# 64-column products between 32-column attention sums: two column groups in place of four

## The chip, the cores and the metric

The kernel runs on one core of a Trainium2 chip. The time is the device time of one execution in microseconds, the median of several runs; less is better. The engines are named as the profile names them: PE is TensorE's matmul and PEld its weight load, DVE is VectorE, ACT ScalarE, POOL GpSimd, SP SyncE.

## The reference

An input x of shape (2, 256, 128, 128), f32: two batches, 256 times T, 128 bands FB, 128 channels C. Three steps, each added to x:

```python
xt = _ln(x, ln_t_w, ln_t_b).transpose(0, 2, 1, 3)
x = x + _mha(xt, t_wi, t_bi, t_wo, t_bo, H_T, cm).transpose(0, 2, 1, 3)   # over time, causal
xf = _ln(x, ln_f_w, ln_f_b)
x = x + _mha(xf, f_wi, f_bi, f_wo, f_bo, H_F, bm)                         # over bands, |i - j| <= 16
xn = _ln(x, ln_n_w, ln_n_b)
h = jax.nn.gelu(xn @ w1.T + b1, approximate=False)                        # 128 -> 512
x = x + (h @ w2.T + b2)                                                   # 512 -> 128
```

`_mha` has 4 heads of 32 channels: `qkv = x @ wi.T + bi`, softmax of scaled and masked scores, times v, and an output product with `wo`.

## The kernel before

All of the work is done in groups of 512 tokens (four tiles of 128): 128 groups over time (class `OverTime`), 128 over bands (`OverBands`) and 128 of the feed-forward part (`FeedForward`). First come all groups over time; then sixteen runs, each of eight groups over bands followed by eight of the feed-forward part.

A group has normalized and transposed tokens `xnT` (128 channels on the partitions, 512 tokens). Its matmuls, all in f32:

- `queries_keys` makes queries and keys, weights `wf` in the array, 512 tokens moving (in the profile `bank<-xnT,wf`).
- `values` makes values, the tokens in the array and `wf` moving, 128 columns for each tile (`bank<-wf,xnT`). Over time, tiles 1 and 3 (`swapped`) have the two halves of their tokens exchanged, by the argument `turn`.
- the scores of a head use 32 rows and 64 columns of the array (`bank<-qT,kT`); over time in an order written out by hand, over bands with 80 moving columns for each 64 keys.
- `weigh` makes the sums of the softmax with a block of ones (`bank<-p,ones` over time, `bank<-pf,ones` over bands) and the weighted values (`bank<-p,v`, `bank<-pf,v`), 128 rows and 32 columns, each head in its own 32 columns.
- `output` makes the output product with `wn` (`bank<-wn,oT`), 128 moving columns a tile.
- in the feed-forward part `hidden` multiplies by `w1f` (512 moving, `bank<-xnT,w1f`) and `weigh` by `w2T_sb` (128 moving, `bank<-w2T_sb,hT`), summed over four parts of the hidden layer.

Queries, keys, values, outputs and both feed-forward products go through one helper, `product`. It writes 128 output partitions in several matmuls side by side, each into a part of the array's columns, with all 128 rows.

Each engine has one queue, worked off in the order in which the program issues (`InOrder` pins it); the loop in `BoundedPath.run` writes that order out. Stages of neighbouring groups are interleaved. In a step over time PE does: the scores of two groups, the output product of an earlier one, sums and weighted values of another, projections of a later one, and the scores again. In a step over bands: scores, sums, weighted values, output product, projections, scores. A feed-forward step has hidden products, second products and hidden products again; its first steps still finish the last band groups, its last ones start the next run's.

PSUM has eight banks, handed on by number (`bank_108` to `bank_115` in the order below). A second path, `shifted_path`, is for inputs whose scores could be too large for a softmax without a maximum; it isn't executed on this input.

All the instructions are issued by one wrapper, so the profile puts nearly all of them on its line, L907: tile names, not lines, tell them apart.

Of the kernel before, what the change touches and what calls it, by code (L numbers as in the profile page):

```python
# [19 lines left out]
P = 128  # L20
H = 4
D = 32
# [3 lines left out]
NT = 4  # L26
# [7 lines left out]
HALF = P // 2  # L34
# [335 lines left out]
class Group:  # L370
# [150 lines left out]
    def values(self):  # L521
        pass
# [38 lines left out]
class Attention(Group):  # L561
# [9 lines left out]
    def queries_keys(self):  # L571
        path = self.path
        wf = path.k.wf[self.which]
        self.qp = path.bank([P, NT * P], "qp", self.place.get("qp", path.held.pop("qp", None)))
        product(path, self.qp, wf[:, 0:P], self.xnT)

        self.kp = path.bank([P, NT * P], "kp", self.place.get("kp"))
        product(path, self.kp, wf[:, P : 2 * P], self.xnT)
# [11 lines left out]
    def values(self):  # L590
        path = self.path
        wv = path.k.wf[self.which][:, 2 * P : 3 * P]
        self.vp = path.bank([P, NT, P], "vp", self.place.get("vp"))
        for i in range(NT):
            product(path, self.vp[:, i], self.xnT[:, i * P : (i + 1) * P], wv, turn=2 if i in self.swapped else 0)

    def take_values(self):
        path = self.path
# [43 lines left out]
def rows_of(h):  # L642
    return slice(h * D, (h + 1) * D)


def product(path, out, weights, x, start=True, stop=True, turn=0):


    for c in range(P // D):
        path.tensor.matmul(out[rows_of(c)], weights[:, rows_of((c + turn) % NT)], x, start=start, stop=stop)  # L650


class OverTime(Attention):
# [7 lines left out]
    def values(self):  # L661
        path = self.path
        wv = path.k.wf[self.which][:, 2 * P : 3 * P]
        self.vp = [path.bank([P, 2, P], "vp", self.place.get(f"vp{s}")) for s in range(2)]
        for i in range(NT):
            product(
                path, self.vp[i // 2][:, i % 2], self.xnT[:, i * P : (i + 1) * P], wv, turn=2 if i in self.swapped else 0
            )

    def take_values(self):  # L670
# [842 lines left out]
```

## Time and profile before

| | |
|---|---|
| median of 3 runs | 2633.39 us (2633.3 to 2634.98) |
| span of the profiled execution, first to last instruction | 2631.9 us |
| what lies around the span, against the lowest run | 1.4 us |
| PE busy | 2617.8 us (99%), 68688 matmuls |
| PE weight loads busy | 1837.4 us (70%), 68688 loads |
| DVE / ACT / POOL busy | 2140.8 (81%) / 1838.8 (70%) / 1958.6 (74%) us |
| granted TensorE clock, mean | 1.000 |

No time of its own is listed for the profiled execution besides its span, so the span stands beside the runs. Busy time is the time in which at least one instruction of an engine or group is running; matmuls overlap, so the busy times of groups add up to more than the engine's. A mean duration is that of one instruction from its start to the end of its results, with the way through the array; how fast matmuls follow one another is read from the starts in the timeline, where instructions of one kind in a row are merged. A form such as 128\*32 is rows\*columns of the array that an instruction uses.

### The profile page before, as it was taken

To read this page: it belongs to the slowest core of one execution; us is meant where nothing else is said; L and a number is where in the kernel's file an instruction comes from. 1 tells how busy PE (TensorE), PEld (TensorE's weight loads), DVE (VectorE), ACT (ScalarE), POOL (GpSimd) and SP (SyncE) were. 2 spreads that over 40 slices of the span, in tenths; PEclk is the share of its full clock that TensorE was granted. 3 is DMA by queue.
4 is the path that set the end of the run, shared out by engine and by line. 5 is a ranking of instruction groups with operands and counts; after the bars stand their busy time and mean duration, and the time that the engine had idled before them with its cause. 6 is when DMAs were issued, how large, how long until landed. Compare 5 with 4: busy or idle time off the path is not lost.

```text
span 2631.9 us, 156460 instructions
## 1 busy us (share of the span) xinstructions
PE 2617.8 (99%) x68688; PEld 1837.4 (70%) x68688; DVE 2140.8 (81%) x6410; ACT 1838.8 (70%) x3543; POOL 1958.6 (74%) x2311
## 2 busy tenths in 40 slices
PE   9999999999999999999999999999999999999999
PEld 6666666666766767666777776667676677777776
DVE  8888888888888887977878779788797797887974
ACT  7989988999899875564655746647557466475573
POOL 7999999999999987666667666665776666757762
PEclk9999999999999999999999999999999999999999
DMA  6656555565565454445454544554454445554543
GB/s 155 167 149 158 149 149 149 155 155 149 149 158 149 122 127 119 115 123 127 118 124 124 123 122 117 126 128 120 122 126 120 120 119 131 123 120 123 123 104 88
DMA packets 469797, 344.97 MB, mean 131 GB/s; under 512 B 43120, under 2 KB 404464, under 8 KB 469104
## 3 DMA queue, kind: packets, MB, share of 16 engines
q1 hardware_dynamic: 468408, 334.41, 50.5%
q8 instruction: 540, 8.85, 1.5%
q14 instruction: 153, 1.25, 0.2%
q10 hardware_dynamic: 696, 0.46, 0.1%
HBM read 167.98 MB, written 166.72 MB: 127 GB/s over the span
## 4 chain that ended last, share of the span: by engine, by line
PE 99%; DVE 0%; issue 0%; DMA 0%; ACT 0%; ACTq 0%; DVEq 0%
PE bank L907 99%; DMA x<-in_x 0%; DVE xh L907 0%; DVE bank L907 0%; DVE res L907 0%; DVE stats L907 0%; DVE oT L907 0%; DVE u L907 0%; DVE xnT L907 0%; ACTq L907 0%; ACT p L907 0%; DVE vy L907 0%; ACT lnv L907 0%; DVE mv L907 0%; ACT root L907 0%
## 5 line engine op out<-in xcount | busy, mean ns | idle before, releaser
L907 ACT ACTIVATE hT<-bank,b 128x512 f32<-128x512 f32 x512 | 348.1, 688 | 524.2 <-PE bank L907 483.2
L907 POOL TENSOR_SCALAR_AFFINE_SELECT pf<-pf 128x512 f32<-128x512 f32 x768 | 477.7, 637 | 185.3 <-ACT pf L907 159.1
L907 PEld LDWEIGHTS bank<-w2T_sb,hT 128*32 128x32 f32 x16384 | 467.4, 110 | 54.8 <-issue 29.0
L907 PE MATMUL bank<-xnT,wf 128*32 128x512 f32 x4096 | 492.4, 592 | 0.5 <-DVE xnT L907 0.5
L907 PE MATMUL bank<-xnT,w1f 128*32 128x512 f32 x4096 | 486.3, 592 | 0.2 <-issue 0.2
L907 PE MATMUL bank<-w2T_sb,hT 128*32 128x128 f32 x16384 | 482.8, 273 | 1.0 <-issue 1.0
L907 ACT ACTIVATE p<-bank 128x512 f32<-128x512 f32 (+1 forms) x1024 | 430.6, 494 | 62.9 <-PE bank L907 62.9
L907 DVE TENSOR_SCALAR xh<-x,mv,rstd 128x160 f32<-128x160 f32 (+1 forms) x1012 | 394.3, 432 | 59.7 <-POOL rstd L907 49.4
L907 POOL TENSOR_SCALAR_AFFINE_SELECT p<-p 128x1024 f32<-128x1024 f32 (+2 forms) x384 | 364.5, 949 | 57.5 <-ACT p L907 49.1
L907 PEld LDWEIGHTS bank<-wf,xnT 128*32 128x32 f32 x8192 | 243.3, 110 | 144.1 <-issue 101.6
L907 POOL TENSOR_TENSOR p<-p,p 128x512 f32<-128x512 f32 x256 | 324.6, 1291 | 10.6
L907 DVE BATCH_NORM_STATS2 stats<-x 128x6 f32<-128x128 f32 x1536 | 329.0, 276 | 3.4 <-DMA x<-in_x 3.4
L907 POOL TENSOR_SCALAR rstd<-mv 128x4 f32<-128x4 f32 x251 | 57.8, 230 | 361.7 <-DVE mv L907 360.5
L907 PEld LDWEIGHTS bank<-xnT,w1f 128*32 128x32 f32 x4096 | 183.6, 110 | 171.6 <-issue 109.6
L907 PE MATMUL bank<-qT,kT 32*64 32x80 f32 (+4 forms) x16384 | 302.0, 271 | 0.1
L907 PEld LDWEIGHTS bank<-qT,kT 32*64 32x64 f32 x16384 | 260.0, 131 | 51.2 <-ACT kT L907 50.6
L907 DVE TENSOR_TENSOR res<-bank,res 128x512 f32<-128x512 f32 (+1 forms) x259 | 170.3, 658 | 153.3 <-PE bank L907 144.7
L907 ACT ACTIVATE pf<-bank 128x512 f32<-128x512 f32 x512 | 265.8, 602 | 35.5 <-PE bank L907 31.3
L907 PE MATMUL bank<-wn,oT 128*32 128x128 f32 x8192 | 283.8, 274 | 0.1
L907 DVE STREAM_TRANSPOSE z<-xh 128x512 f32<-128x512 f32 x380 | 270.3, 711 | 13.3
L907 PE MATMUL bank<-wf,xnT 128*32 128x128 f32 x8192 | 276.5, 273 | 0.0
L907 POOL TENSOR_TENSOR rstd<-rstd,mhalf 128x4 f32<-128x4 f32 x251 | 260.8, 1039 | 20.9
(100 smaller groups left out, 3820.3 us busy)
## 6 DMA issues: line engine op xcount, KB each, us to landing
turned<-z SPq DMA_DIRECT2D x1520, 64.0 KB, 2.7
xnT<-turned SPq DMA_DIRECT2D x380, 256.0 KB, 3.2
x<-res SPq DMA_DIRECT2D x256, 128.0 KB, 2.5
x<-x SPq DMA_DIRECT2D x128, 256.0 KB, 4.1
out<-res SPq DMA_DIRECT2D x252, 128.0 KB, 2.3
x<-in_x SPq DMA_DIRECT2D x124, 256.0 KB, 4.3
x<-in_x SPq DMA_DIRECT2D x4, 128.0 KB, 2.8
x<-in_x SPq DMA_DIRECT2D x6, 64.0 KB, 2.9
```

The lines of the kernel that those rows point to most:

```text
L907: return self.tc.keep_in_program_order(emit(*args, **kwargs))
```

## The change

`product` splits its 128 output columns into two halves of 64 in place of four quarters of 32, and so issues two matmuls where it issued four. With two halves the exchange of token halves is `turn=1` in place of `turn=2`; which tokens land where stays the same. Sums, weighted values and scores have matmuls of their own and keep their forms.

```diff
@@ Attention.values @@
-            product(path, self.vp[:, i], self.xnT[:, i * P : (i + 1) * P], wv, turn=2 if i in self.swapped else 0)
+            product(path, self.vp[:, i], self.xnT[:, i * P : (i + 1) * P], wv, turn=1 if i in self.swapped else 0)
@@ product @@
-    for c in range(P // D):
-        path.tensor.matmul(out[rows_of(c)], weights[:, rows_of((c + turn) % NT)], x, start=start, stop=stop)
+    for c in range(2):
+        w = (c + turn) % 2
+        path.tensor.matmul(
+            out[c * HALF : (c + 1) * HALF], weights[:, w * HALF : (w + 1) * HALF], x, start=start, stop=stop
+        )
@@ OverTime.values @@
-                path, self.vp[i // 2][:, i % 2], self.xnT[:, i * P : (i + 1) * P], wv, turn=2 if i in self.swapped else 0
+                path, self.vp[i // 2][:, i % 2], self.xnT[:, i * P : (i + 1) * P], wv, turn=1 if i in self.swapped else 0
```

The order of the stages stays as it was on every engine of the executed path; what changes is which matmuls PE finds in it. PE's order in a step over time, before, from the end of the scores to the start of the next ones (out<-in, output partitions x moving columns, how many in a row):

```order
L907 MATMUL bank_115<-qT,kT 64x64
L907 MATMUL bank_108<-wn_236,oT 32x128 x16
L907 MATMUL bank_114<-p_6843,ones 32x2x128 x4
L907 MATMUL bank_114<-p_7001,ones 32x2x128 x4
L907 MATMUL bank_113<-p_6843,v 32x256 x4
L907 MATMUL bank_113<-p_7001,v 32x128 x4
...
L907 MATMUL bank_109<-xnT,wf_151 32x512 x4
L907 MATMUL bank_112<-xnT,wf_151 32x512 x4
L907 MATMUL bank_108<-wf_151,xnT 32x128 x8
L907 MATMUL bank_115<-wf_151,xnT 32x128 x8
L907 MATMUL bank_110<-qT,kT 64x64
```

The same place in PE's order after the change:

```order
L910 MATMUL bank_115<-qT,kT 64x64
L910 MATMUL bank_108<-wn_224,oT 64x128 x8
L910 MATMUL bank_114<-p_6015,ones 32x2x128 x4
L910 MATMUL bank_114<-p_6153,ones 32x2x128 x4
L910 MATMUL bank_113<-p_6015,v 32x256 x4
L910 MATMUL bank_113<-p_6153,v 32x128 x4
...
L910 MATMUL bank_109<-xnT,wf_151 64x512 x2
L910 MATMUL bank_112<-xnT,wf_151 64x512 x2
L910 MATMUL bank_108<-wf_151,xnT 64x128 x4
L910 MATMUL bank_115<-wf_151,xnT 64x128 x4
L910 MATMUL bank_110<-qT,kT 64x64
```

The output product and the projections have half as many matmuls of twice the columns; the sums and weighted values between them keep 32. Before, everything between the two sets of scores had one form; now it has two, and changes from 64 to 32 and back.

PE's order in a step over bands, before, from the sums to the next scores:

```order
L907 MATMUL bank_108<-pf,ones 32x512 x4
L907 MATMUL bank_109<-pf,v 32x128 x16
L907 MATMUL bank_114<-wn_241,oT 32x128 x16
L907 MATMUL bank_115<-xnT,wf_238 32x512 x4
L907 MATMUL bank_110<-xnT,wf_238 32x512 x4
L907 MATMUL bank_111<-wf_238,xnT 32x128 x16
L907 MATMUL bank_112<-qT,kT 64x80
```

And after the change:

```order
L910 MATMUL bank_108<-pf,ones 32x512 x4
L910 MATMUL bank_109<-pf,v 32x128 x16
L910 MATMUL bank_114<-wn_229,oT 64x128 x8
L910 MATMUL bank_115<-xnT,wf_226 64x512 x2
L910 MATMUL bank_110<-xnT,wf_226 64x512 x2
L910 MATMUL bank_111<-wf_226,xnT 64x128 x8
L910 MATMUL bank_112<-qT,kT 64x80
```

Here one change is new, from the weighted values (32 columns) to the output product (64). The feed-forward steps consist of products alone and have one form throughout, 64 in place of 32. The instructions of DVE, ACT, POOL and SP, and their waits, stay in their order.

## The prediction

> **What bounds the kernel.** I read the head of the page first, then the chain that ended last, then the groups of instructions by form, and then the timeline of TensorE (PE) around single stages.
>
> ```profile
> span 2631.9 us, 156460 instructions
> PE 2617.8 (99%) x68688; PEld 1837.4 (70%) x68688; DVE 2140.8 (81%) x6410; ACT 1838.8 (70%) x3543; POOL 1958.6 (74%) x2311
> PEclk9999999999999999999999999999999999999999
> PE 99%; DVE 0%; issue 0%; DMA 0%; ACT 0%; ACTq 0%; DVEq 0%
> ```
>
> PE is the bound, at the full granted clock, over the whole span: it is 99% busy and makes up 99% of the chain that ended last. So whatever the change adds to PE's stream or takes from it appears in the time, and no other engine need be priced as long as it isn't pushed past PE; the next, DVE, stands at 81%. But a busy PE is not the same as a PE at its peak, so the stream itself has to be read. Its groups, with every shape apart (tile names, rows*columns of the array used, moving operand, count, busy time in all, mean ns of one):
>
> ```profile
> L907 PE MATMUL bank<-xnT,wf 128*32 128x512 f32 x4096 | 492.4, 592 | 0.5 <-DVE xnT L907 0.5
> L907 PE MATMUL bank<-xnT,w1f 128*32 128x512 f32 x4096 | 486.3, 592 | 0.2 <-issue 0.2
> L907 PE MATMUL bank<-w2T_sb,hT 128*32 128x128 f32 x16384 | 482.8, 273 | 1.0 <-issue 1.0
> L907 PE MATMUL bank<-wn,oT 128*32 128x128 f32 x8192 | 283.8, 274 | 0.1
> L907 PE MATMUL bank<-wf,xnT 128*32 128x128 f32 x8192 | 276.5, 273 | 0.0
> L907 PE MATMUL bank<-qT,kT 32*64 32x80 f32 x8192 | 124.0, 240 | 0.1
> L907 PE MATMUL bank<-ident,xh 128*128 128x128 f32 x32 | 4.7, 291 | 1.0 <-DVE xh L907 1.0
> L907 PEld LDWEIGHTS bank<-w2T_sb,hT 128*32 128x32 f32 x16384 | 467.4, 110 | 54.8 <-issue 29.0 <-ACT hT L907 10.9 <-ACT waste L907 0.3
> L907 PEld LDWEIGHTS bank<-qT,kT 32*64 32x64 f32 x16384 | 260.0, 131 | 51.2 <-ACT kT L907 50.6 <-ACT p L907 0.2 <-DVE oT L907 0.2
> L907 PEld LDWEIGHTS bank<-ident,xh 128*128 128x128 f32 x32 | 4.0, 190 | 2.0 <-DVE xh L907 1.4 <-DVE mv L907 0.4
> ```
>
> The first five rows are what the change touches, 40960 matmul records: each f32 matmul of the program leaves two records. PE runs them today in one form of the array, 128*32, which the softmax sums and weighted values also have; the scores alone are 32*64. Now one attention group over time, then one over bands (start, duration with tail, count):
>
> ```profile
> 700.19 1.39 PE L907 MATMUL bank<-qT,kT 32*64 32x64 f32 x64
> 701.50 1.08 PE L907 MATMUL bank<-wn,oT 128*32 128x128 f32 x32
> 702.40 1.05 PE L907 MATMUL bank<-p,ones 128*32 128x256 f32 x16
> 703.26 1.48 PE L907 MATMUL bank<-p,v 128*32 128x256 f32 x32
> 704.56 1.90 PE L907 MATMUL bank<-xnT,wf 128*32 128x512 f32 x16
> 706.28 1.06 PE L907 MATMUL bank<-wf,xnT 128*32 128x128 f32 x32
> 707.27 1.39 PE L907 MATMUL bank<-qT,kT 32*64 32x64 f32 x64
> ```
>
> ```profile
> 1497.43 0.97 PE L907 MATMUL bank<-qT,kT 32*64 32x80 f32 x64
> 1498.33 1.06 PE L907 MATMUL bank<-pf,ones 128*32 128x512 f32 x8
> 1499.21 1.06 PE L907 MATMUL bank<-pf,v 128*32 128x128 f32 x32
> 1500.08 1.06 PE L907 MATMUL bank<-wn,oT 128*32 128x128 f32 x32
> 1500.95 1.90 PE L907 MATMUL bank<-xnT,wf 128*32 128x512 f32 x16
> 1502.67 1.06 PE L907 MATMUL bank<-wf,xnT 128*32 128x128 f32 x32
> 1503.66 0.97 PE L907 MATMUL bank<-qT,kT 32*64 32x80 f32 x64
> ```
>
> Go by the starts. Thirty-two records of 128 columns take 0.87 us (1499.21 to 1500.08, and again to 1500.95): eight passes of four side by side, 0.109 us a pass. Sixteen of 512 columns take 1.72 us: four passes of 0.430. The slope between them is (0.430 - 0.109) / 384 = 0.83 ns a column, so a pass costs its columns and under 3 ns more. Nothing else is paid as long as the form stays: pf,ones, pf,v, wn,oT and xnT,wf follow one another without a gap.
>
> Where the form changes, something is paid. wf,xnT to the scores takes 0.99 us (1502.67 to 1503.66, 706.28 to 707.27) where its eight passes take 0.87: 0.12 of nothing. And the first stage behind the scores is too long by about 0.025: wn,oT at 701.50 takes 0.90 in place of 0.87, pf,ones 0.88 in place of 2 x 0.430.
>
> **What the change does to a pass.** Two records of 64 columns stand in the place of four of 32. The product forms go from 40960 records to 20480, with as many passes: (16384 + 8192 + 8192) / 4 = 8192 of 128 columns and 8192 / 4 = 2048 of 512. What a pass costs with two groups and 128 rows isn't in the trace. The nearest rows, with their loads:
>
> ```profile
> 25.50 1.16 PE L907 MATMUL bank<-ident,xh 128*128 128x128 f32 x8
> 26.39 0.28 PE L907 MATMUL bank<-ident,xh 128*128 128x128 f32 x1
> 26.59 0.40 PE L907 MATMUL bank<-p,ones 128*32 128x256 f32 x1
> 13.08 0.38 PE L907 MATMUL bank<-ident,xh 128*128 128x128 f32 x1
> 13.19 0.86 PEld L907 LDWEIGHTS bank<-ident,xh 128*128 128x128 f32 x7
> 2000.18 0.13 PEld L907 LDWEIGHTS bank<-xnT,wf 128*32 128x32 f32 x4 [0.30 <-ACT pf L907]
> 2000.61 0.13 PEld L907 LDWEIGHTS bank<-xnT,wf 128*32 128x32 f32 x4 [0.30 <-issue]
> ```
>
> The full array, one group of 128, is one end: seven loads in 0.86 us, so (0.86 - 0.19) / 6 = 0.112 a pass of 128 columns. Four groups are the other, at 0.109. The loads tell which one is nearer. With four groups a bundle of four loads is over in 0.13 us and then nothing is loaded for 0.30, while the pass of 0.43 runs: the next weights wait behind the matmul. With the full array a load is as long as the pass (128 columns each, no idle time between the loads at 13.19), so there the load sets the pace. A load of 64 lies between the means of 110 and 190 ns, at 131 in the scores, and isn't as long as any pass here. I take 0.109, no gain and no loss, in all feed-forward products too, which are most of the edit. The cover is the matmul of the pass before.
>
> TensorE: Matmul & The Clock Gate of the Trainium skill (Part 3, The mechanism) says that a weight load runs beside matmuls in flight only where the row group differs. Here every load of the 128*32 forms uses all row groups and is hidden all the same, so by these rows the rule doesn't hold for this kernel; it is priced below as a rival.
>
> **What it does between passes.** Products are now 128*64, sums and weighted values stay 128*32, scores 32*64: three forms where there were two. I counted changes of form in PE's order of the built programs: 524 before, 921 after. The 397 new ones:
> - over time, output product to sums (wn,oT to p,ones), 64 to 32: 126
> - over time, weighted values to projections (p,v to xnT,wf), 32 to 64: 126
> - over bands, weighted values to a product (pf,v to wn,oT or xnT,wf), 32 to 64: 128
> - the last band group's sums inside the feed-forward run (w1f to pf,ones), 64 to 32: 16
> - and one at the start.
>
> Their price: first the drain. In all changes above rows and columns change together; here only the columns do. The two rows at 26.39 and 26.59 are such a change, 128*128 to 128*32: 0.20 us from the last matmul to the next, of which its 128 columns at 0.83 are 0.107, so 0.09 are lost. The change to the scores shows the same from four groups:
>
> ```profile
> 1503.43 0.29 PE L907 MATMUL bank<-wf,xnT 128*32 128x128 f32 x4
> 1503.66 0.28 PE L907 MATMUL bank<-qT,kT 32*64 32x80 f32 x1
> ```
>
> From the first of the last four to the first score 0.23 us in place of 0.109: 0.12 lost, more than 0.09 since the last of four starts some 0.02 behind the first (0.29 for four, 0.27 for one). I take 0.115 out of four groups and, with a skew of a third of that, 0.10 out of two.
>
> TensorEngine Tiling (Array Packing) of the Trainium skill (Tiling Modes, Key Properties) states that changing the tiling mode, though not just the tile, drains TensorE. The trace agrees, with 0.09 to 0.12 us each time. It is the rule that speaks against this change: by it the sum is the one below, without it nothing is left.
>
> Second, the first load in the new form can't hide behind a pass. It shows as 0.025 us for 32 columns (above), and as 0.10 for 128: the first ident,xh at 13.08 takes 0.38, the one at 26.39 takes 0.28. For 64 columns the first score takes 0.28 against a mean of 0.24 that contains such first ones. I take 0.05, in proportion to the columns; the ends are 0.025 and 0.10.
>
> The sum, by stage:
> - A group over time: 0.10 + 0.025 into the sums, 0.115 + 0.05 into the projections; the output product behind the scores loads 64 columns in place of 32, +0.025; the exit to the scores leaves two groups in place of four, -0.013. In all 0.30 us; 7.08 us (700.19 to 707.27) become 7.38. Times 126: 38.
> - A group over bands: 0.165 - 0.013 = 0.15; 6.23 us (1497.43 to 1503.66) become 6.38. Times 128: 19.5.
> - A feed-forward run: 0.125 into the sums and 0.025 for the larger first load behind the scores. Times 16: 2.4.
>
> Together 60 us, on 2631.9 gives 2692. The runs shown have a median of 2633.4, 1.5 more than the profiled span; with that the forecast is 2693 us, 2.3% slower. A change below 0.2%, 5.3 us, can hardly be told from none here.
>
> Off the path: operations, order and waits on DVE, ACT, POOL and SP are those of before, and no transfer is moved. Behind each drain stand the sums, the projections and the scores, with ACT and DVE waiting for their banks; they get everything 0.3 us later in 7, and with shares of 70 to 81% they have the slack to follow. Half the records spare PE's sequencer work, but that bound nothing: four starts lie within some 0.02 us, and a pass takes 0.109.
>
> **Rivals.**
> - Columns alone don't drain: with all 128 rows in both forms, PE could go from 32 to 64 as from one product to the next. Then the 397 new changes cost nothing, and the two small terms of the old ones cancel (140 x 0.025 - 256 x 0.013 = 0): 2633, not slower. It decides below 5.3 / 397 = 13 ns a change. The rows at 26.39 and 26.59 speak against it, with 0.09. 4 in 100.
> - Two groups pace like the full array, 0.112 in place of 0.109 a pass: 10240 x 0.0024 (from the unrounded 0.1117 that seven passes between 25.50 and 26.39 give less the first load) = 25 us more: 2718. For it: fewer groups to alternate between. Against it: there the load is as long as the pass. 9 in 100.
> - The pass gets shorter, because the under 3 ns belong to the four records: at most 10240 x 0.0026 = 27 us, so 2666; still slower. The 0.430 for 512 columns shows how little there is to win. 4 in 100.
> - Weight loads come out from behind the matmuls: 10240 x 0.05 = 512 us more, some 3200. The hidden loads of today, all rows in each, speak against it. 1 in 100.
>
> **Numbers.** My forecast has 80 in 100, at 2693; 2 in 100 are for what I don't see. Within it the first load of 64 columns moves 395 entries (255 new, 140 old) by -0.025 or +0.05: 2683 to 2713. The drain between 0.09 and 0.12 moves 397 changes by some 5 us. The slower pace at 2718 is just taken in: 2680 to 2719. Faster by over 0.2% would need a mechanism that I don't find: 2 in 100; within 0.2%, the first rival: 4; slower: 94.
>
> **What would show it.** PE records fall by 20480 to about 48208. In the timeline 128*64 passes of 128 columns still come every 0.109 us and of 512 every 0.43. wn,oT to p,ones and p,v to xnT,wf grow by 0.10 and 0.115, the stages behind by 0.025 and 0.05; a group over time takes 7.38, over bands 6.38. The feed-forward stretches between attention runs keep their time. I am wrong if stages of both forms follow without a gap, or if the feed-forward part changes its time by more than a few us.

## The result and the profile after

The changed kernel takes 2679.32 us, the kernel before 2634.18 in the same runs: a ratio of 1.017 with a 95% interval of 1.0155 to 1.0184. It is slower, as forecast, by 45 us where 60 were forecast, and ends 0.7 us below the range.

The head of its page and its queue of instructions (packets, MB, share), and ahead of them the same queue before:

```profile
q8 instruction: 540, 8.85, 1.5%
```

```profile
span 2676.4 us, 115500 instructions
PE 2667.1 (100%) x48208; PEld 1769.5 (66%) x48208; DVE 2140.9 (80%) x6410; ACT 1846.8 (69%) x3543; POOL 1952.2 (73%) x2311
q8 instruction: 380, 6.23, 1.0%
```

PE has the 48208 records of the forecast and is still the bound. Its timeline in a step over time, a step over bands and the feed-forward part:

```profile
696.68 1.39 PE L910 MATMUL bank<-qT,kT 32*64 32x64 f32 x64
698.00 1.09 PE L910 MATMUL bank<-wn,oT 128*64 128x128 f32 x16
699.02 1.07 PE L910 MATMUL bank<-p,ones 128*32 128x256 f32 x16
699.91 1.48 PE L910 MATMUL bank<-p,v 128*32 128x256 f32 x32
701.32 1.94 PE L910 MATMUL bank<-xnT,wf 128*64 128x512 f32 x8
703.09 1.04 PE L910 MATMUL bank<-wf,xnT 128*64 128x128 f32 x16
704.06 1.39 PE L910 MATMUL bank<-qT,kT 32*64 32x64 f32 x64
...
1190.27 1.07 PE L910 MATMUL bank<-pf,ones 128*32 128x512 f32 x8
1191.15 1.06 PE L910 MATMUL bank<-pf,v 128*32 128x128 f32 x32
1192.14 1.09 PE L910 MATMUL bank<-wn,oT 128*64 128x128 f32 x16
1193.06 1.89 PE L910 MATMUL bank<-xnT,wf 128*64 128x512 f32 x8
...
2000.89 3.66 PE L910 MATMUL bank<-w2T_sb,hT 128*64 128x128 f32 x64
2004.39 3.60 PE L910 MATMUL bank<-xnT,w1f 128*64 128x512 f32 x16
2007.82 3.66 PE L910 MATMUL bank<-w2T_sb,hT 128*64 128x128 f32 x64
```

A step over time takes 7.38 us (696.68 to 704.06), to the digit what was forecast. The output product takes 1.02 in place of 0.90, p,v 1.41 in place of 1.30, the first projections 1.77 in place of 1.72. Over bands pf,v takes 0.99 in place of 0.87, and wn,oT behind it 0.92. In the feed-forward part 32 passes take 3.50 us and eight of 512 columns 3.43: 0.109 and 0.429 a pass. So the changes of form cost what the prediction said, and still 15 us are missing from the sum.

They are in the kernel before. I took each of PE's stretches of one form, from its first matmul to the first of the next form, and took off its passes and the fixed price of the entry (0.135 us into 128\*32, 0.150 into 128\*64; of the 399 stretches of 128\*64 after the change, nine in ten lie between 0.146 and 0.151). After the change 1.2 us are left over, in three places. Before, 15.8 us are left over, in 47. The balance: 400 x 0.150 + 256 x 0.135 - 259 x 0.135 = 59.6 us of entries, less 14.6 of waits that went, is 45.0; the two spans are 44.5 apart.

### The profile page after: what moved, and what is told of

Its sections match the earlier page's. It is cut to its first block, busy times and chain, and to the rows that moved or that the text cites. A ratio compares the mean times of both kernels' runs of the same rounds, so it can differ in the third digit from the quotient of the medians.

```text
span 2676.4 us, 115500 instructions
## 1 busy us (share of the span) xinstructions
PE 2667.1 (100%) x48208; PEld 1769.5 (66%) x48208; DVE 2140.9 (80%) x6410; ACT 1846.8 (69%) x3543; POOL 1952.2 (73%) x2311
## 4 chain that ended last, share of the span: by engine, by line
PE 99%; DMA 0%; DVE 0%; issue 0%; ACT 0%; ACTq 0%; DVEq 0%
PE bank L910 99%; DMA xnT<-turned 0%; DMA x<-in_x 0%; DVE stats L910 0%; DVE xnT L910 0%; ACTq L910 0%; ACT p L910 0%; DVE xh L910 0%; DVE vy L910 0%; ACT lnv L910 0%; DVE res L910 0%; DVE mv L910 0%; ACT root L910 0%; DVE rstd L910 0%; DVEq L910 0%
## 5 line engine op out<-in xcount | busy, mean ns | idle before, releaser
L910 PEld LDWEIGHTS bank<-w2T_sb,hT 128*64 128x64 f32 x8192 | 454.6, 137 | 65.9 <-issue 64.0
L910 PE MATMUL bank<-xnT,wf 128*64 128x512 f32 x2048 | 490.3, 599 | 1.0 <-DVE xnT L910 0.5
L910 PE MATMUL bank<-w2T_sb,hT 128*64 128x128 f32 x8192 | 469.7, 273 | 0.0
L910 PE MATMUL bank<-xnT,w1f 128*64 128x512 f32 x2048 | 466.8, 592 | 0.0
L910 PEld LDWEIGHTS bank<-wf,xnT 128*64 128x64 f32 x4096 | 241.3, 137 | 146.1 <-issue 145.8
L910 PE MATMUL bank<-wn,oT 128*64 128x128 f32 x4096 | 279.5, 279 | 0.1
L910 DVE TENSOR_TENSOR bank<-bank,r 128x512 f32<-128x512 f32 x240 | 166.8, 695 | 134.4 <-PE bank L910 113.5
L910 PEld LDWEIGHTS bank<-xnT,w1f 128*64 128x64 f32 x2048 | 141.5, 137 | 200.4 <-issue 182.7
```

The lines of the kernel that those rows point to most:

```text
L910: return self.tc.keep_in_program_order(emit(*args, **kwargs))
```

## Where the waits of before are

Two places in the timeline of the kernel before (in brackets, PE's idle time ahead and what ended it):

```profile
368.35 1.25 PE L907 MATMUL bank<-p,v 128*32 128x256 f32 x20
370.86 0.63 PE L907 MATMUL bank<-p,v 128*32 128x256 f32 x8 [1.26 <-issue]
...
1173.99 1.05 PE L907 MATMUL bank<-pf,v 128*32 128x128 f32 x30
1175.87 0.30 PE L907 MATMUL bank<-pf,v 128*32 128x128 f32 x1 [0.83 <-issue]
```

PE stops in the middle of a stage and waits for nothing that the profile shows. In PE's list of waits it is the first row (us, times, longest); after the change the list has no such row:

```profile
PE bank L907 <- issue: 4.4, 9, 1.3
```

What it waits for shows when its records are numbered from 0 in order of their starts, matmuls, loads and the 510 of its sequencer together. The instruction queue carries blocks of 16 KB (8.85 MB in 540 packets; 160 fewer after the change, and 40960 fewer records of PE: 256 a block). The longest of these stops end at a record whose number is 193 modulo 256: 370.86 at record 19393, 1175.87 at 62657. Each ends 1.2 to 1.8 us after a packet of that queue has landed, and for record 256 k + 193 it is always the k-th packet. Twenty gaps over 0.1 us have both marks at this one place; with those one record off they add up to some 9 us. After the change no place stands out: before, such a record starts 1.2 us behind its packet at the least, after the change 2.4. So such a stop is PE out of instructions, since the next block came late.

Runtime: NRT & Kernel Launch of the Trainium skill (Instruction fetch mechanics) says that each engine streams its instructions in blocks of 16 KiB, 256 instructions, and that crossing into the next is mostly hidden. The trace agrees with the block. Of the 538 borders here all but those twenty show no such gap; in a run below, with more instructions, 522 of 730 have one, and there the crossing isn't mostly hidden.

Most of the other 7 us are regular. In nearly every one of the sixteen runs the stretches that begin with the sums of the sixth and of the seventh band group come out 0.1 and 0.2 to 0.3 us late. These are waits for GpSimd's masks. The seventh group's sums and the later half of their weight loads, before, and in another run the seventh group's sums after the change:

```profile
2457.99 1.39 PE L907 MATMUL bank<-pf,ones 128*32 128x512 f32 x8
2458.32 0.14 PEld L907 LDWEIGHTS bank<-pf,ones 128*32 128x32 f32 x4 [0.19 <-POOL pf L907]
```

```profile
1222.17 1.06 PE L910 MATMUL bank<-pf,ones 128*32 128x512 f32 x8
```

Before, GpSimd ends the last mask of these two groups 0.02 and 0.23 us (medians of the sixteen runs) after PE has started their sums. After the change it ends them 0.35 and 0.19 us before.

## Experiments

Theory A: the changes of form cost what was forecast, and the waits of before go, since PE has half the product instructions to fetch and reaches the other engines' results later. B: before lost nothing, and a change of form costs 45 / 397 = 0.114 us. C: it isn't the changes of form; a pass of 64 columns is slower.

**Sums and weighted values at 64 too.** In `weigh`, each loop over four heads:

```diff
-            for h in range(H):
-                w = self.p1[:, :, h, 1] if n else self.p0[:, :, h, 0:P]
-                path.tensor.matmul(rp[rows_of(h), :, n], path.k.ones[:, 0:D], w, start=True, stop=True)
+            for c in range(2):
+                w = self.p1[:, :, 2 * c, 1] if n else self.p0[:, :, 2 * c, 0:P]
+                path.tensor.matmul(rp[half_of(c), :, n], path.k.ones[:, 0:HALF], w, start=True, stop=True)
```

> The changed kernel, with the softmax sums and weighted values in two groups of 64 columns too. Heads 1 and 3 are left out of them: heads 0 and 2 are computed into their rows. So PE has as many passes as before, 42576 records in place of 68688, and 524 changes of form, as many as before. Theory A (the changes of form cost what the prediction said, 0.135 us an entry into 32 columns and 0.150 into 64; but the kernel before lost some 16 us at PE, waiting for blocks of its own instructions that came late, and half the records end that): 2580.9 us of stream and scores + 259 x 0.150 = 2620 us of span, 2622 us of time, 12 us faster than before. Theory B (before lost nothing, a change of form is simply cheaper, 45 us / 397 = 0.114): no more changes than before, so 2634 us, the time of before. Theory C (a pass of 64 columns is itself slower): some 2679, as the changed kernel.

2628.45 us against 2636.78, a ratio of 0.9974 (0.9963 to 0.9984): faster than before. A step over time, from the sums on:

```profile
700.90 1.03 PE L914 MATMUL bank<-p,ones 128*64 128x256 f32 x8
701.77 1.47 PE L914 MATMUL bank<-p,v 128*64 128x256 f32 x16
703.07 1.89 PE L914 MATMUL bank<-xnT,wf 128*64 128x512 f32 x8
704.78 1.04 PE L914 MATMUL bank<-wf,xnT 128*64 128x128 f32 x16
```

Without a change of form p,v takes 1.30 again. C is out: all passes are now two groups, and the 45 us are gone. B falls too, since it has no way below the time of before. A forecast 2622 and missed by 6: 7.0 us of waits stay, and none is at a border of a block. 5.5 us of them are the regular ones, 0.10 and 0.27 us in a run; the rest are two longer ones, near the start and in the first run.

**More instructions, the same work.** Products of 512 moving columns are issued as four of 128, with four groups of 32 and with two of 64:

```diff
-        product(path, self.qp, wf[:, 0:P], self.xnT)
+        quarters(path, self.qp, wf[:, 0:P], self.xnT)   # and for the keys and the hidden products
+def quarters(path, out, weights, x):
+    for i in range(NT):
+        product(path, out[:, i * P : (i + 1) * P], weights, x[:, i * P : (i + 1) * P])
```

> The kernel before (four groups of 32), with every product of 512 moving columns issued as four of 128: the same columns stream through PE, the forms change as often as before, but PE has 93264 records in place of 68688, all at the pace of 0.109 us for four. 6144 more passes cost 6144 x 0.0026 = 16 us. Theory A: 256 instructions then last some 3.5 us nearly everywhere, less than a block of them took to come where before stalled, so waits appear at the borders of blocks throughout: over 2700 us, perhaps 2900. Theories B and C, in which instructions don't matter: 2634 + 16 = 2650.

> The changed kernel (two groups of 64) with the same split of 512 moving columns into four of 128: 60496 PE records, still fewer than before, 921 changes of form. Theories A, B and C alike: 2679 + 16 = 2695; by A, no waits at the borders of blocks, since 256 instructions last over 5 us.

With four groups 2978.79 us, a ratio of 1.1298 (1.1271 to 1.1326). The page, PE's longest wait (us, times, longest), and a place:

```profile
span 2982.2 us, 205612 instructions
PE 2778.8 (93%) x93264; PEld 2424.6 (81%) x93264; DVE 2159.4 (72%) x6410; ACT 1849.8 (62%) x3543; POOL 1960.2 (66%) x2311
q8 instruction: 732, 11.99, 1.8%
...
PE bank L912 <- issue: 184.2, 324, 2.2
...
1227.18 0.43 PE L912 MATMUL bank<-xnT,w1f 128*32 128x128 f32 x8
1229.30 3.48 PE L912 MATMUL bank<-xnT,w1f 128*32 128x128 f32 x120 [1.69 <-issue]
1232.57 3.71 PE L912 MATMUL bank<-w2T_sb,hT 128*32 128x128 f32 x128
```

The columns are the same and the passes 16 us more, yet 350 us are added to the span. A had over 2700, perhaps 2900, B and C 2650. Now 522 gaps over 0.1 us stand at record 193 modulo 256 and end 1.1 to 1.8 us behind a landed block. With two groups the same split gives 2694.2 us, as forecast, and PE's list of waits has no such row. So the number of instructions alone makes PE wait, at the borders of blocks: the dose of what before had a little of. This shows the mechanism; that 9 of the 15 us of the change are this is from the place of the gaps in the trace.

**Feed-forward or attention alone.** `product` gets the number of groups as an argument; first only the feed-forward products have two, then only projections and outputs.

> Only the two feed-forward products in two groups of 64; projections and output products stay at four of 32. 634 changes of form (before 524, changed 921), 58448 PE records. Theory A: 2580.9 + 305 x 0.135 + 64 x 0.150 = 2632 us of span, and some 8 of the 16 us that before lost stay, in the attention steps: 2640, 2642 us of time. Theory B: 2634 + 110 x 0.114 = 2646.5. Theory C: the feed-forward steps have 6144 of the 10240 passes of 64, so 2634 + 0.6 x 45 = 2661.

2647.18 us, a ratio of 1.0039 (1.0025 to 1.0053), 5 above A's number and at B's. A's entries hold; its waits don't: I let 8 us stay, and 13.6 did, 7 of them at borders of blocks. C's 2661 is out.

> Only projections and output products in two groups of 64; the feed-forward products stay at four of 32. 999 changes of form, more than the 921 of the whole change, since now feed-forward steps and output products differ too. Theory A: 2580.9 + 430 x 0.150 + 304 x 0.135 = 2686 us of span, and the late instruction blocks and waits of the feed-forward runs stay in part, 2 to 6 us: about 2690 to 2694 of time, slower than the whole change. Theory B: 2634 + 475 x 0.114 = 2688. Theory C (a pass of 64 is slower): 0.4 of the 45 us, 2652.

2693.52 us (one round, two executions), 14 more than the whole change: the feed-forward steps in two groups save changes of form beside attention steps in two. A holds; B isn't far off; C's 2652 is out.

**Two groups only inside the feed-forward run.** The number of groups is switched to two at the second hidden step and back before the next run's projections, which costs two changes of form a run.

> Two groups of 64 from the second hidden step of a feed-forward run to its last one, with the one output product among them; everything else at four of 32. 556 changes of form (before 524) and 59472 records (before 68688). Theory A: 2580.9 + 274 x 0.135 + 17 x 0.150 = 2620.5 us of span without waits, and of the 16 us of waits in the kernel before those of the attention steps stay, 10 to 13: 2631 to 2634, 2632.5 to 2636 of time, the same as before within what can be told. Theory B: 2634 + 32 x 0.114 = 2638.

2640.95 us, a ratio of 1.002 (1.0011 to 1.0029). Not the same as before but at the edge of what can be told, on the slow side, and 5 us above A. It has 9216 records fewer than before and yet 18.9 us of waits, 9.5 of them at borders. So fewer instructions in the feed-forward part don't help: the late blocks fall into attention steps and between the parts, where 256 instructions pass quickest. Which border is hit shifts with every edit; I can't forecast it to better than some 5 us.

**The price of a change of form.** The output product over time is moved behind the weighted values, in the changed kernel and in the one before:

```diff
-                do(n - 2, "output")
...
-            if old is not None:
-                do(n - 2, "finish")
...
             do(n - 1, "weigh")
+            if old is not None:
+                do(n - 2, "output", "finish")
```

> The changed kernel with one thing moved: in a step over time the output product is issued behind the sums and weighted values, beside the projections, which have its form. Passes and records as in the changed kernel; 796 changes of form in place of 921. Theory A (an entry into 64 columns costs 0.150 us in all, with the load that can't hide): 125 entries less, -19 us: 2658 us of span, 2660 of time. Theory B (0.114 a change): 2679 - 14 = 2665. If the changes of form weren't the cost, 2679. The other order may bring waits of its own; the same order in the kernel before shows them.

> The kernel before (four groups of 32) with the same move of the output product behind sums and weighted values. Forms, records and changes of form (524) as before, so by all theories the time of before, 2635, but for waits that the order itself makes.

2755.32 and 2730.53 us. Both forecasts of the time missed, because the order makes waits of its own, at the scores. PE's first wait in the list of the changed kernel, then its first two in that of the kernel before:

```profile
PE bank L910 <- ACT p L910: 72.7, 125, 0.6
```

```profile
PE bank L907 <- ACT p L907: 63.4, 109, 0.6
PE bank L907 <- POOL p L907: 9.3, 16, 0.6
```

These waits for p add up to 72.7 us in both, and the stretches of one form have 0.6 and 14.1 us left over, much as the 1.2 and 15.8 without the move. So against each other the two still tell the price: the spans are 2753.1 and 2728.2, 24.9 apart in place of 44.5. The 125 entries taken away were worth 19.6 us, 0.157 each, where A has 0.150 and B 0.114.

**The regular waits.** Half of the band masks are left out (`for s in (1,)` in place of `(1, -1)`), in the kernel before and in the first experiment's.

> The kernel before with half of the band masks left out: GpSimd makes one affine_select in place of two for each of three heads, so the sums over bands get their input earlier. PE's own stream isn't touched. If the regular waits at the sums of the first feed-forward step (some 0.27 us in each of the 16 runs) are waits for GpSimd, they go: 2631.9 - 16 x 0.27 = 2628 us of span, 2629 to 2630 of time, and the irregular waits for instruction blocks (some 9 us) stay. If all of the 16 us were late blocks, nothing changes: 2634.

> Sums and weighted values in two groups of 64 (heads 1 and 3 left out of them, as in the run of that name), and half of the band masks left out too. There were no late blocks there, but regular waits, in each run 0.10 us in one band step and 0.27 in the first feed-forward step, 6 us in all. If the 0.27 are waits for GpSimd's masks they go: 2626.3 - 4.2 = 2622 us of span, 2624 of time. If they have another cause, 2626 and 2628.

2635.05 us against 2634.35 (ratio 0.9999, 0.9989 to 1.001), and 2624.53 (0.9964, 0.9951 to 0.9976). In both traces the masks of the sixth and seventh group now end over 1.6 us before PE starts their sums, and both regular waits at these sums are gone. So they were waits for GpSimd. In the same stretch, 16 us later, another wait comes in, at an output product in the feed-forward run:

```profile
1095.60 0.53 PEld L914 LDWEIGHTS bank<-wn,oT 128*64 128x64 f32 x10 [0.90 <-DVE oT L914]
```

It waits for oT, the last band group's weighted values, which DVE divides there. The loads stand idle for 0.90 us, PE itself loses 0.18, and so in each run, 2.9 us in all. The second kernel meets the forecast of 2624 with some luck: the 0.10 went too, which it had not counted, and the new waits took more than that back. For the first kernel the forecast missed. Eleven such waits for oT come in, 2.0 us, and its late blocks fall elsewhere again and are more (26 gaps at record 193 in place of 20).

So PE meets the waits for GpSimd only if it comes early; after the change, with 0.15 us more in each band step, it finds the masks ready. That the delay of PE is the reason is read from the trace after; I made no run that slows PE alone.

No version that computes everything beat the kernel before.

## Why the prediction was wrong

- PE as the bound, with passes of 0.109 and 0.43 us that stay with two groups: right. The load of 64 columns stays hidden in all of the feed-forward part.
- The drain for a change of columns alone: right. From the end of the last matmul's columns to the next form's first matmul both new kinds of change take 0.095 us, as the old ones do. The first load of 64 shows 0.05, as taken. The 397 changes and the steps of 7.38 us came out as forecast; a feed-forward pass kept its time.
- The sum: wrong by 15 us, in the paragraph "Off the path", with two terms put at nothing. First, "Half the records spare PE's sequencer work, but that bound nothing": I looked at the starts in a pass, 0.02 us for four, and not at where the instructions come from. Some 9 us of before were waits for late blocks of instructions. The term was set to zero and measured 9.
- Second, "no other engine need be priced as long as it isn't pushed past PE": the sum let the others follow with their slack and gave nothing for that slack. GpSimd, busy for 74% of the span, already held PE up at two places in each run, some 6 us, and coming later PE met its masks ready. This term too was set to zero.
- So the range was built of the bounds of new costs alone. It had no term for what before lost and the change could end, and its lower end, 2680, left no room there. The profile had shown it: the 4.4 us of "PE bank L907 <- issue", and stages in the timeline longer than their passes. I checked a few regular steps and never added up all of them against the span.
- The rivals: a free change of columns is out, by the 0.095; the full array's pace, a shorter pass and exposed loads are out, by the passes.

## What to carry to other kernels

Price a change of PE's tiling by its entries: about 0.095 us of drain, also where only the columns change, and the first load in the new form, uncovered. Before a forecast goes on a span that is 99% busy, add up what the stages should take and compare: what is left over are waits, and a change that makes the bound engine slower or its instructions fewer gives them back. Where it has many small matmuls, PE can run out of instructions: with 93264 records in place of 68688 the span grew by 350 us here.

## What the runs showed of the hardware

- PE took 256 instructions in some 3.5 us, where all matmuls have 128 columns in four groups, only as long as the blocks kept up. With 732 blocks in 2982 us, one every 4.07, they didn't, and PE stood still for up to 2.2 us at a time.
- A stopped PE goes on 1.1 to 1.8 us after the block's packet has landed, 1.4 in the median.
- The uncovered first load is proportional to its columns: 25, 51 and 102 ns for 32, 64 and 128.
- One, two or four column groups give nearly the same f32 pass: 0.112, 0.109 and 0.109 us for 128 columns.
